# A fused cross-attention block in fp32: the pipeline's fifth step in an order of its own, and three smaller moves

## The chip, the cores and the metric

The kernel runs on one NeuronCore of one Trainium2 chip. The metric is the device time of one launch in microseconds. Each launch reads its inputs from the chip's memory (HBM) and writes the output there. TensorE is called PE in the profile, VectorE DVE, ScalarE ACT, GpSimd POOL, and SyncE, which does nothing here but issue transfers, SP.

## What is computed

For 128 batches of 128 tokens with 256 features, in fp32: 16-head attention of `x` on a second sequence `ctx`, whose mask lets token i see only tokens j < i, and whose row 0 is set to zero; the output projection, a residual and a layer norm; then a feed-forward block of 1024 hidden units with relu, a residual and a second layer norm.

```python
q = (x @ Wq + bq);  k = (ctx @ Wk + bk);  v = (ctx @ Wv + bv)      # 16 heads of 16
scores = where(j < i, q @ k.T / 4, -1e30)
attn = softmax(scores);  attn[:, :, 0, :] = 0
x1 = layer_norm(x + (attn @ v) @ Wo + bo, g1, be1)
out = layer_norm(x1 + relu(x1 @ W1 + b1) @ W2 + b2, g2, be2)
```

## The kernel before, in words

The work is cut into 64 pairs of batches, p = 0 to 63, and everything is written out by hand: each engine runs its instructions in the order in which the Python code emits them, and waits by semaphores where data or a buffer is not ready. So the order of the calls in `third`, `fourth`, `fifth`, `step` and `behind` is the order on every engine, and on SP the order in which transfers are issued.

A call of `step(p)` (L1114) handles four pairs at different stages:

- `weigh(p-2)` (L465) multiplies the older pair's transposed probabilities `pT` with its values into the PSUM tile `pc`, and `context` (L495) copies the result to `cxT` on ACT.
- `scores_both(p)` (L351) makes the scores `pss`. A query in the upper half of the tokens sees all 128 keys ("high", hi = 1), one in the lower half only 64 ("low"). The eight PSUM banks have fixed uses: high scores in banks 0 to 3, low scores in 6, 7, 4, 5.
- `mask`, `mask_high`, `low_maximum` (L377, L728, L742) add the mask and find the maxima on DVE; `exponential_by_head` (L746) makes 32 exponentials on ACT, the high ones straight from PSUM; `sums` (L405) adds them up on DVE and scales them on POOL.
- `queries(p+1)`, `keys(p+1)`, `values(p)` (L267, L277, L288) are the projections, each with PE products into a fixed bank (4, 0, 1) and copies by ACT (`qT`, `kT`, and `vz`, `vd` in `values_out`, L298).
- `attention_out(p-2)`, `attention_sum`, `attention_stats`, `shift`, `norm1` (L499 to L552) are the output projection `po` and the first layer norm.
- `hidden(p-3)` (L680) multiplies with W1 into `ph` and applies relu on ACT into `hT`. It needs the normalized tokens with features on the partitions, `x1T`: `turn_x1` (L652) transposes 32x32 blocks on DVE (`tbx`), and SP writes them to HBM in four transfers (`x1t`, L239) and reads them back in one (`x1T`, L242).
- `second_by_seven(p-4)` (L775) multiplies with W2 in seven quarter products instead of eight (Strassen's scheme in Winograd's form). `combine_hidden` (L764) makes the four sums of hidden blocks that it needs (`hS`), on two engines that are passed in. `sum_of_seven` (L803) adds the products up. `second_half` (L825) is the plain form for the first pairs.
- `turn(p, hi, t)` (L422) transposes blocks of the probabilities on DVE into the tile `tb`, in three calls for a pair: `(p,1,0)`, `(p,1,1)`, `(p,0,0)`. `bring` (L435) then issues sixteen transfers on SP that move `tb` to `pT`, the layout that `weigh` reads. Each reads columns that all three calls have written.
- `norm2`, `finish`, `store` (L579, L587, L597) are the second layer norm on ACT and POOL and the output transfer.

`sm` (scores and probabilities), `tb` and `pT` share four large buffers in turn (`wide`, L317), in the order in which the tiles are first asked for.

`empty(n)` (L213) puts n empty instructions into PE's stream. The kernel has 44 of them ahead of its first product (L839), which is a warm-up of twelve transposes of the identity, and one within each of the seven W2 products.

The first pairs are too early for this pattern. `third`, `fourth` and `fifth` (pairs 2, 3, 4) have orders of their own. The call `step(5)` has branches for `p == 5`: the store of pair 0, the second half of `hidden(2)`, `second_half(2, 0)`. `step(6)` has `second_half(2, 1)`. Behind the last pair, `behind(62)` and `behind(63)` (L1186) and some lines of their own finish the rest; there `combine_hidden` is split between DVE and POOL (`BOTH`).

The line numbers here and in the profile are those of the kernel before.

Of the kernel before, what the change touches and what calls it, by code (L numbers as in the profile page):

```python
# [19 lines left out]
def tile_cross_attention_block(  # L20
# [237 lines left out]
    def project(w, src, ps):  # L258
        for m in range(KC):
            for k in range(KC):  # L260
                nc.tensor.matmul(  # L261
                    ps[:, m * TP : (m + 1) * TP], w[:, k, m * P : (m + 1) * P], src[:, k, :],
                    start=(k == 0), stop=(k == KC - 1),
                )
        return ps
# [9 lines left out]
            )  # L275

    def keys(p):  # L277
        st = states[p]
        st["kT"] = proj.tile([P, KC, 2, TP], F32, tag="kT", name=f"kT_{p}")
        pk = project(wk, st["cT"], at_bank(0, f"pk_{p}") if p > 3 else bank(f"pk_{p}"))  # L280
        for m in range(KC):
            for e in range(2):
                nc.scalar.activation(  # L283
                    st["kT"][:, m, e, :], pk[:, m * TP : (m + 1) * TP], AF.Identity,
                    bias=bkh[:, m, e : e + 1], scale=half[:, e : e + 1],
                )

    def values(p):  # L288
        st = states[p]
        pv = st["pv"] = at_bank(1, f"pv_{p}") if p > 3 else bank(f"pv_{p}")  # L290
        for s in range(2):
            for k in range(KC):
                nc.tensor.matmul(  # L293
                    pv[:, s * D : (s + 1) * D], st["cT"][:, k, s * P : (s + 1) * P], wv[:, k, :],
                    start=(k == 0), stop=(k == KC - 1),
                )
# [300 lines left out]
    def store(p):  # L597
        nc.sync.dma_start(
            out[2 * p : 2 * p + 2].rearrange("b p d -> p b d"), states.pop(p)["t2"]
        )  # L600
# [76 lines left out]
            else:  # L677
                nc.scalar.copy(st["x1T"][:, :, :, k, :], pt[:, k])

    def hidden(p, fs, between=None):  # L680
        st = states[p]
        if fs[0] == 0:
            st["hT"] = ffn.tile([P, FC, TP], F32, tag="hT", name=f"hT_{p}", bufs=1)
        for f in fs[::2]:
            if p == 0:
                ph = bank(f"ph_{p}_{f}")
            else:
                ph = at_bank((2, 3, 4, 0)[f // 2], f"ph_{p}_{f}")
            for i in range(2):
                for k in range(KC):  # L690
                    nc.tensor.matmul(  # L691
                        ph[:, i * TP : (i + 1) * TP].rearrange("p (s i a) -> p s i a", s=2, a=32),
                        w1[:, k, (f + i) * P : (f + i + 1) * P], st["x1T"][:, :, :, k, :],
                        start=(k == 0), stop=(k == KC - 1),
                    )
            for i in range(2):
                nc.scalar.activation(  # L697
                    st["hT"][:, f + i, :], ph[:, i * TP : (i + 1) * TP], AF.Relu,
                    bias=(b1e_c if p else b1_c)[:, f + i : f + i + 1], scale=1.0,
                )  # L700
            if between:
                between(f)
# [133 lines left out]
        nc.vector.tensor_tensor(st["t2"][:, s], py[:, :D], st["x1b"][:, s], ALU.add)  # L836

    warm = bank("warm")
    empty(44)  # L839
    for i in range(12):  # L840
        nc.tensor.transpose(warm[:, i % 4 * P : (i % 4 + 1) * P], ident, ident)
    states[0] = {}
# [193 lines left out]
    def fourth():  # L1036
        p = 3
        load_ahead(p)
        scores(p, 1)
        mask(p, 1, A)  # L1040
        maximum(p, 1, ONE)
        second(0, 0)
        mask(p, 1, B)
        maximum(p, 1, TWO)
        exponential(p, 1, ONE)
        second(0, 1)
        tokens(p + 2, "c")
        sums(p, 1, ONE)
        exponential(p, 1, TWO)
        second_sum(0)  # L1050
        sums(p, 1, TWO)
        weigh(p - 1)
        context(p - 1)
        scores(p, 0)
        scale_w1()
        nc.gpsimd.tensor_tensor(b1e_c, b1e_c, b1_c, ALU.add)
        queries(p + 1)
        mask(p, 0, A)
        mask(p, 0, B)
# [12 lines left out]
        turn_x1(p - 1)  # L1072
        turn(p, 0, 0)
        bring(p, nc.sync, LATE_FIRST)
        stats(0, states[0]["t2"], 2)
        scale_and_shift(0)
        norm2(0)

    def fifth():
        p = 4  # L1080
        load_ahead(p)
        scores_both(p)
        mask(p, 0, B)
# [30 lines left out]
    def step(p):  # L1114
        last = p == NP - 1
        weigh(p - 2)
        context(p - 2)
        scores_both(p)
        if p > 6:
            combine_hidden(p - 4, POOL_ALONE)  # L1120
        if p == 5:
            second_sum(1)
            finish(0)
            store(0)
# [9 lines left out]
        if p > 5:  # L1134
            exponential_by_head(p, 0, range(H))
# [9 lines left out]
        if p == 5:  # L1145
            exponential_by_head(p, 0, range(H))
        values(p)
        values_out(p)
        if p > 5:
            norm2(p - 5)  # L1150
        sums(p, 1, ONE)
        sums(p, 1, TWO)
        sums(p, 0, ALL)
        turn_x1(p - 2)
        residual1(p - 3)
        if p > 6:
            second_by_seven(p - 4)
        elif p == 6:
            second_half(2, 1)
        hidden(p - 3, range(FC // 2 if p == 5 else 0, FC))  # L1160
        if p == 5:
            second_half(2, 0)
# [9 lines left out]
        if p > 5:  # L1172
            finish(p - 5)
            store(p - 5)
# [6 lines left out]
    for p in range(5, NP):  # L1181
# [96 lines left out]
```

## Time and profile before

| | us |
|---|---|
| median of 3 timed runs | 1550.86 (1549.78 to 1553.15) |
| time of the profiled execution | 1548.3 |
| its span, first to last instruction | 1546.2 |
| TensorE busy in it | 1518.6 (98%) |
| mean granted TensorE clock | 0.995 of full speed |

A row of the timeline has the start and the length in us, the engine, the line, the operation, the tile written and the tiles read, and how many instructions were merged; a bracket at its end gives the engine's idle time before the row and what is taken to have ended it. `SPq` rows are transfers being issued, not moved. A row of the waits has the waiting engine and tile, the releaser, the sum in us, the number of times and the longest. PEld is TensorE's weight load, which runs ahead of the products (PE), so its waits for the same thing can be longer.

### The profile page before, as it was taken

Reading aid. Unit: us, or ns where it says so; the run is one execution under the profiler, and the core shown is the slowest. Engines: PE = TensorE matmul, PEld = TensorE weight load, DVE = VectorE, ACT = ScalarE, POOL = GpSimd, SP = SyncE. Lnnn points to the kernel's source line nnn. Section 1 sums busy time; section 2 is a strip of 40 time slices with the busy share of each in tenths; the row PEclk is TensorE's granted clock in tenths of the full one; section 3 lists DMA queues with packets and bytes.
Section 4 is the critical chain, followed back from the end, with each engine's and each line's share of the span. In section 5 each row is a group of like instructions: output and inputs, shape, how many; then the busy total and the mean of one; then the engine's idle time right before and its main releaser. Section 6 shows DMA issues by size and latency. Waiting matters only on the chain.

```text
span 1546.2 us, 47890 instructions
## 1 busy us (share of the span) xinstructions
PE 1518.6 (98%) x17926; PEld 1362.5 (88%) x17926; DVE 1329.0 (86%) x2490; ACT 1119.8 (72%) x3391; POOL 1265.3 (82%) x1290
## 2 busy tenths in 40 slices
PE   8997999999999999999999999999999999999998
PEld 6786899899899899899899899899899899899887
DVE  6987889889889889889889889889898898898864
ACT  5666778778778778778778777777777777777752
POOL 6875888888888888888888888888888888888874
PEclk9998999999999999999999999999999999999999
DMA  8355666566556556556566566566566566555431
GB/s 198 77 116 125 145 133 143 124 139 143 138 134 147 124 135 146 138 137 147 117 141 147 133 138 135 135 136 150 132 136 140 127 137 151 131 132 130 107 94 48
DMA packets 415285, 204.24 MB, mean 132 GB/s; under 512 B 282448, under 2 KB 383056, under 8 KB 415056
## 3 DMA queue, kind: packets, MB, share of 16 engines
q1 hardware_dynamic: 413152, 200.13, 56.2%
q8 instruction: 144, 2.36, 0.7%
q10 hardware_dynamic: 1904, 1.06, 0.3%
q14 instruction: 85, 0.70, 0.2%
HBM read 70.26 MB, written 33.29 MB: 67 GB/s over the span
## 4 chain that ended last, share of the span: by engine, by line
PE 92%; POOL 3%; DVE 3%; issue 1%; ACT 1%; DMA 0%; POOLq 0%; DVEq 0%
PE ph L691 27%; PE py L784 13%; PE pz L784 10%; PE pq L261 8%; PE po L504 7%; PE pk L261 7%; PE pv L293 7%; PE pss L368 6%; PE pc L485 3%; PE pc L475 2%; POOL sm L415 1%; PE py L709 0%; DVE tb L428 0%; DVE sm L382 0%; POOL sd L525 0%
## 5 line engine op out<-in xcount | busy, mean ns | idle before, releaser
L691 PE MATMUL ph<-x1T,w 128*128 128x256 f32 x2048 | 455.6, 380 | 3.0 <-ACT kT L283 3.0
L691 PEld LDWEIGHTS ph<-x1T,w 128*128 128x128 f32 x2048 | 385.4, 191 | 54.3 <-ACT kT L283 3.4
L415 POOL TENSOR_TENSOR sm<-sm,rs 128x1024 f32<-128x1024 f32 x192 | 359.4, 1899 | 7.1 <-ACT hT L697 4.5
L752 ACT ACTIVATE sm<-pss,nmx 128x128 f32<-128x128 f32 x944 | 249.8, 415 | 131.5 <-DMA pT<-tb 84.5
L697 ACT ACTIVATE hT<-ph,b1e_c 128x256 f32<-128x256 f32 x504 | 209.5, 467 | 179.3 <-PE ph L691 179.1
L752 ACT ACTIVATE sm<-sm,nmx 128x64 f32<-128x64 f32 x944 | 231.8, 334 | 5.2
L413 DVE TENSOR_REDUCE su<-sm 128x8 f32<-128x1024 f32 (+1 forms) x192 | 225.9, 1176 | 9.4 <-ACT sm L752 5.6
L428 DVE STREAM_TRANSPOSE tb<-sm 128x1024 f32<-128x1024 f32 x186 | 220.8, 1214 | 0.0
L382 DVE TENSOR_TENSOR sm<-pss,neg 128x256 f32<-128x256 f32 (+1 forms) x276 | 108.3, 436 | 126.2 <-PE pss L368 118.6
L524 POOL TENSOR_SCALAR ve<-mv 128x2 f32<-128x2 f32 x127 | 29.4, 231 | 205.4 <-DVE mv L518 204.9
L784 PE MATMUL py<-wt,hS 128*128 128x128 f32 x1440 | 171.4, 275 | 3.1 <-POOL hS L771 3.1
L784 PEld LDWEIGHTS py<-wt,hS 128*128 128x128 f32 x1440 | 165.8, 192 | 3.7 <-POOL hS L771 3.7
L737 DVE TENSOR_REDUCE nmx<-pss 128x4 f32<-128x512 f32 x236 | 150.9, 681 | 0.0
L261 PE MATMUL pq<-xT,wq 128*128 128x256 f32 x504 | 127.2, 395 | 5.2 <-DVE sm L382 5.2
L283 ACT ACTIVATE kT<-pk,bkh,half 128x256 f32<-128x256 f32 x252 | 120.2, 557 | 3.9 <-PE pk L261 3.9
L293 PE MATMUL pv<-wv,cT 128*128 128x256 f32 x512 | 121.1, 379 | 1.6 <-ACT sm L752 1.6
L504 PE MATMUL po<-wo,cxT 128*128 128x256 f32 x512 | 121.2, 379 | 0.0
L261 PE MATMUL pk<-cT,wk 128*128 128x256 f32 x504 | 119.2, 379 | 0.0
L261 PEld LDWEIGHTS pq<-xT,wq 128*128 128x128 f32 x504 | 91.7, 192 | 26.0 <-issue 10.1
L293 PEld LDWEIGHTS pv<-wv,cT 128*128 128x128 f32 x512 | 97.1, 190 | 15.1 <-ACT sm L752 2.0
L504 PEld LDWEIGHTS po<-wo,cxT 128*128 128x128 f32 x512 | 97.0, 190 | 13.8 <-ACT cxT L497 0.3
L261 PEld LDWEIGHTS pk<-cT,wk 128*128 128x128 f32 x504 | 95.7, 190 | 13.1 <-issue 0.2
(131 smaller groups left out, 2971.5 us busy)
## 6 DMA issues: line engine op xcount, KB each, us to landing
pT<-tb SPq DMA_DIRECT2D x984, 96.0 KB
x1t<-tbx SPq DMA_DIRECT2D x252, 64.0 KB
x1T<-x1t SPq DMA_DIRECT2D x63, 256.0 KB
out_dram<-t SPq DMA_DIRECT2D x63, 256.0 KB
xb<-in_x_dram SPq DMA_DIRECT2D x124, 128.0 KB
cb<-in_ctx_dram SPq DMA_DIRECT2D x124, 128.0 KB
x<-in_x_dram SPq DMA_DIRECT2D x31, 512.0 KB
w<-in_L_xattn_W_dram SPq DMA_DIRECT2D x2, 1024.0 KB
```

The costliest lines, as they stand in the source:

```text
L261: nc.tensor.matmul(ps[:, m * TP : (m + 1) * TP], w[:, k, m * P : (m + 1) * P], src[:, k, :], start=(k == 0), stop=(k == KC - 1),)
L283: nc.scalar.activation(st["kT"][:, m, e, :], pk[:, m * TP : (m + 1) * TP], AF.Identity, bias=bkh[:, m, e : e + 1], scale=half[:, e : e + 1],)
L293: nc.tensor.matmul(pv[:, s * D : (s + 1) * D], st["cT"][:, k, s * P : (s + 1) * P], wv[:, k, :], start=(k == 0), stop=(k == KC - 1),)
L413: nc.vector.tensor_reduce(su, sm[:, part, :], AX.X, ALU.add)
L415: nc.gpsimd.tensor_tensor(sm[:, part, :], sm[:, part, :], rs[:, :, None].to_broadcast([P, part.stop - part.start, n]), ALU.mult,)
L428: nc.vector.transpose(st["tb"][:, :, at : at + 256].rearrange("p j (n a) -> p n j a", a=32), st["sm", hi].rearrange("p h j -> p (h j)")[:, ...
L504: nc.tensor.matmul(po[:, s * D : (s + 1) * D], cxT[:, k, s, :], wo[:, k, :], start=(k == 0), stop=(k == KC - 1),)
L691: nc.tensor.matmul(ph[:, i * TP : (i + 1) * TP].rearrange("p (s i a) -> p s i a", s=2, a=32), w1[:, k, (f + i) * P : (f + i + 1) * P], st[ ...
L697: nc.scalar.activation(st["hT"][:, f + i, :], ph[:, i * TP : (i + 1) * TP], AF.Relu, bias=(b1e_c if p else b1_c)[:, f + i : f + i + 1], sc ...
L737: nc.vector.tensor_reduce(st["nmx", 1][:, 4 * r : 4 * r + 4], st["sps", 1][r].rearrange("p (n j) -> p n j", j=P), AX.X, ALU.max, negate=True,)
L752: nc.scalar.activation(sm[:, h, :], src, AF.Exp, bias=nmx[:, h : h + 1], scale=1.0)
L784: nc.tensor.matmul(out, left(k), right(k), start=(k == 0), stop=(k == FC // 2 - 1))
```

## The change

Four things change. Nothing of the arithmetic does, apart from which engine makes some sums.

1. `step(5)` becomes `fall_in(5)`, with an order of its own. In `fifth` only the first of pair 4's three `turn` calls is left; the other two and `bring(4)` come behind `low_maximum(5)`. The low exponentials of pair 5 are split round the two W1 copies, the key copies come behind them (`keys` is cut into `project_keys` and `copy_keys`), and the W1 products use banks 2 and 3. `norm1(3)` comes late, and `turn_x1(3)` is no longer in this step. Two of pair 5's `turn` calls come at its end. In `step(6)`, the third `turn` of pair 5, `bring(5)` and `turn_x1(3)` follow the exponentials of pair 6, in this order.
2. In `fourth`, `queries(4)` comes ahead of `weigh(2)` and not behind `scores(3, 0)`.
3. At the end `combine_hidden` runs on DVE alone, and `finish` and `store` of an older pair come directly behind its `norm2`. In the last pair's step the values use bank 4 and not 1, and the second low mask comes ahead of the high ones.
4. The 44 empty instructions ahead of the warm-up are taken out; 44 are put between pair 1's W1 products, two or three behind each.

```diff
     def values(p):
-        pv = st["pv"] = at_bank(1, f"pv_{p}") if p > 3 else bank(f"pv_{p}")
+        pv = st["pv"] = at_bank(4 if p == NP - 1 else 1, f"pv_{p}") if p > 3 else bank(f"pv_{p}")
...
     def hidden(p, fs, between=None, banks=(2, 3, 4, 0)):
...
+                    if p == 1:
+                        empty(3 if f else 2)
...
-    empty(44)
...
     def fourth():
+        queries(p + 1)
         weigh(p - 1)
         context(p - 1)
         scores(p, 0)
...
-        queries(p + 1)
...
     def fifth():
         turn(p, 1, 0)
-        turn(p, 1, 1)
-        turn(p, 0, 0)
-        bring(p, nc.sync, LATE_FIRST)
         hidden(2, range(FC // 2))
...
+    def fall_in(p):
+        weigh(p - 2)
+        context(p - 2)
+        scores_both(p)
+        second_sum(1)
+        finish(0)
+        store(0)
+        add_bo(p - 1)
+        residual1(2)
+        load_ahead(p)
+        mask(p, 0, B)
+        mask_high(p, A)
+        exponential_by_head(p, 1, ONES)
+        mask_high(p, B)
+        exponential_by_head(p, 1, TWOS)
+        mask(p, 0, A)
+        low_maximum(p)
+        turn(p - 1, 1, 1)
+        turn(p - 1, 0, 0)
+        bring(p - 1, nc.sync, LATE_FIRST)
+        queries(p + 1)
+        exponential_by_head(p, 0, ONES)
+        attention_out(p - 2)
+        attention_sum(p - 2)
+        attention_stats(p - 2)
+        shift(p - 2, 1)
+        project_keys(p + 1)
+        values(p)
+        sums(p, 1, ONE)
+        sums(p, 1, TWO)
+        def between(f):
+            if f == 4:
+                exponential_by_head(p, 0, TWOS[:4])
+        hidden(2, range(FC // 2, FC), between, (2, 3, 2, 3))
+        exponential_by_head(p, 0, TWOS[4:])
+        copy_keys(p + 1)
+        values_out(p)
+        norm1(p - 2)
+        tokens(p + 2, "x")
+        tokens(p + 2, "c")
+        turn(p, 1, 0)
+        sums(p, 0, ALL)
+        turn(p, 1, 1)
+        second_half(2, 0)
+        stats(1, states[1]["t2"], 2)
+        scale_and_shift(1)
...
     def step(p):
+        if last:
+            mask(p, 0, A)
         mask_high(p, A)
...
+        if not last:
+            mask(p, 0, A)
         low_maximum(p)
+        exponential_by_head(p, 0, range(H))
+        if p == 6:
+            turn(p - 1, 0, 0)
+            bring(p - 1, nc.sync, LATE_FIRST)
+            turn_x1(p - 3)
...
-    BOTH = (nc.vector, nc.gpsimd)
+    VECTOR_ALONE = (nc.vector, nc.vector)
     def behind(p):
-        combine_hidden(p - 2, BOTH)
+        combine_hidden(p - 2, VECTOR_ALONE)
         norm2(p - 3)
+        finish(p - 3)
+        store(p - 3)
         second_by_seven(p - 2)
...
-        finish(p - 3)
-        store(p - 3)
...
-    combine_hidden(p - 1, BOTH)
+    combine_hidden(p - 1, VECTOR_ALONE)
```

More of the change, by code (lines that the diff above doesn't have):

```diff
@@ L277, in keys, with project_keys, copy_keys @@
     def keys(p):
+        project_keys(p)
+        copy_keys(p)
+    def project_keys(p):
         st = states[p]
         st["kT"] = proj.tile([P, KC, 2, TP], F32, tag="kT", name=f"kT_{p}")
-        pk = project(wk, st["cT"], at_bank(0, f"pk_{p}") if p > 3 else bank(f"pk_{p}"))
+        st["pk"] = project(wk, st["cT"], at_bank(0, f"pk_{p}") if p > 3 else bank(f"pk_{p}"))
+    def copy_keys(p):
+        st = states[p]
+        pk = st.pop("pk")
         for m in range(KC):
@@ L678, in turn_x1_on_pe, with hidden @@
                 nc.scalar.copy(st["x1T"][:, :, :, k, :], pt[:, k])
-    def hidden(p, fs, between=None):
+    def hidden(p, fs, between=None, banks=(2, 3, 4, 0)):
         st = states[p]
@@ L687, in hidden @@
             else:
-                ph = at_bank((2, 3, 4, 0)[f // 2], f"ph_{p}_{f}")
+                ph = at_bank(banks[f // 2], f"ph_{p}_{f}")
             for i in range(2):
@@ L1112, in tile_cross_attention_block @@
     POOL_ALONE = (nc.gpsimd, nc.gpsimd)
-    def step(p):
-        last = p == NP - 1
+    def fall_in(p):
         weigh(p - 2)
@@ L1118, in step @@
         scores_both(p)
[L1119 to L1124, printed above, removed]
+        second_sum(1)
+        finish(0)
+        store(0)
         add_bo(p - 1)
+        residual1(2)
         load_ahead(p)
@@ L1133, in step @@
         low_maximum(p)
-        if p > 5:
-            exponential_by_head(p, 0, range(H))
+        turn(p - 1, 1, 1)
[27 more added lines that the diff above has]
+        scale_and_shift(1)
+    def step(p):
+        last = p == NP - 1
+        weigh(p - 2)
+        context(p - 2)
+        scores_both(p)
+        if p > 6:
+            combine_hidden(p - 4, POOL_ALONE)
+        add_bo(p - 1)
[15 more added lines that the diff above has]
+            turn_x1(p - 3)
         if not last:
@@ L1144, in step @@
             keys(p + 1)
-        if p == 5:
-            exponential_by_head(p, 0, range(H))
         values(p)
         values_out(p)
-        if p > 5:
-            norm2(p - 5)
+        norm2(p - 5)
         sums(p, 1, ONE)
@@ L1157, in step @@
             second_by_seven(p - 4)
-        elif p == 6:
+        else:
             second_half(2, 1)
-        hidden(p - 3, range(FC // 2 if p == 5 else 0, FC))
-        if p == 5:
-            second_half(2, 0)
+        hidden(p - 3, range(FC))
         if p + 2 < NP:
@@ L1171, in step @@
         bring(p, nc.sync, LATE_FIRST)
-        if p > 5:
-            finish(p - 5)
-            store(p - 5)
+        finish(p - 5)
+        store(p - 5)
         stats(p - 4, states[p - 4]["t2"], 2)
@@ L1180, in tile_cross_attention_block @@
     fifth()
-    for p in range(5, NP):
+    fall_in(5)
+    for p in range(6, NP):
         step(p)
-    BOTH = (nc.vector, nc.gpsimd)
+    VECTOR_ALONE = (nc.vector, nc.vector)
     def behind(p):
```

## The prediction

> **What bounds the kernel now.** I read the page first: the busy times, the clock row and the chain that ended last. Then the busy times by step, a step being one pair of batches, counted from its weigh (the product of an older pair's probabilities and values, first on TensorE).
>
> ```profile
> PE 1518.6 (98%) x17926; PEld 1362.5 (88%) x17926; DVE 1329.0 (86%) x2490; ACT 1119.8 (72%) x3391; POOL 1265.3 (82%) x1290
> ...
> PEclk9998999999999999999999999999999999999999
> ...
> PE 92%; POOL 3%; DVE 3%; issue 1%; ACT 1%; DMA 0%; POOLq 0%; DVEq 0%
> ...
> 106.66:130.00 23.34, 20.33 (x226) 16.86 (x225) 14.08 (x27) 15.81 (x51) 15.40 (x14) 0.85 0.61 136
> 130.00:157.28 27.28, 22.08 (x242) 18.94 (x241) 24.44 (x45) 16.79 (x53) 14.94 (x18) 0.94 0.49 112
> 157.28:180.57 23.29, 23.29 (x282) 21.07 (x281) 20.49 (x39) 17.73 (x55) 20.79 (x21) 1.00 0.62 144
> ```
>
> The last three rows give length, then each engine's busy time and its count, then the granted clock. From 157.28 on a step is 23.29 us of TensorE without a hole, and the change leaves that loop alone. What can move is the start, the steps of pairs 5 and 6 (23.34 and 27.28 us, though each holds less work than a full step, at clocks of 0.85 and 0.94) and the end. The timeline shows where these two steps lose:
>
> ```profile
> 8.53 1.99 PE L865 MATMUL pk<-cT,wk 128*128 128x256 f32 x8
> 116.69 1.89 PE L691 MATMUL ph<-x1T,w 128*128 128x256 f32 x8
> 121.60 3.78 PE L691 MATMUL ph<-x1T,w 128*128 128x256 f32 x8 [3.01 <-ACT kT L283]
> 125.17 4.90 PE L830 MATMUL py<-w,hT 128*128 128x256 f32 x16
> 138.29 3.52 PE L261 MATMUL pq<-xT,wq 128*128 128x256 f32 x8 [5.20 <-DVE sm L382]
> 150.28 7.07 PE L691 MATMUL ph<-x1T,w 128*128 128x256 f32 x32
> ```
>
> The bracket holds the idle time and its releaser. In pair 5's step TensorE waits 3.01 for the copy of the keys, then runs eight products in 3.78 instead of 1.89 and sixteen in 4.90 instead of 3.54 (half of the 7.07 of 32): 3.01 + 1.89 + 1.36 = 6.3 us. In pair 6's step the queries wait 5.20 for VectorE's mask and run in 3.52 instead of 1.99: 6.7 us. So 13 us is the most that the new order can win there.
>
> **The change, part by part.** All times are in the frame of the profiled execution.
>
> *The fifth step.* The new order takes both waits away: the keys are copied behind the W1 results, and VectorE is through with the older pairs before pair 6's masks. TensorE would be done with pair 5's step at 118.4 + 1.8 + 3.5, about 124, instead of 130.0. But the order also moves two transposes of pair 4's probabilities (`turn(4,1,1)`, `turn(4,0,0)`) from ahead of pair 5's masks to behind its `low_maximum`. Each of the sixteen pT transfers of `bring(4)` reads what all three transposes write, so all of `bring(4)` goes with them, and `weigh(4)`, the first work of pair 6's step, needs all sixteen. In the same way `bring(5)` now stands behind `turn(5,0,0)`, behind pair 6's `low_maximum`; and `turn_x1(3)`, whose x1t transfers were issued ahead of `bring(5)` on SP (127.49 against 136.60), is put behind its sixteen. `hidden(3)`, the last work of pair 6's step, needs them. The rows that price this chain (for SP the second column is the time over which the line was issued):
>
> ```profile
> 79.32 2.36 DVE L428 STREAM_TRANSPOSE tb<-sm 128x1024 f32<-128x1024 f32 x2
> 108.94 0.76 DVE L382 TENSOR_TENSOR sm<-pss,neg 128x256 f32<-128x256 f32 x2 [0.90 <-PE pss L368]
> 114.11 1.22 DVE L744 TENSOR_REDUCE nmx<-sm 128x16 f32<-128x1024 f32 x1
> 111.55 1.27 POOL L590 TENSOR_TENSOR t<-t,be_r 128x512 f32<-128x512 f32 x1
> ...
> 65.97 6.03 SPq L443 DMA_DIRECT2D pT<-tb  x8
> 91.69 10.19 SPq L443 DMA_DIRECT2D pT<-tb  x16
> 107.53 11.86 SPq L443 DMA_DIRECT2D pT<-tb  x16
> 119.50 0.52 SPq L598 DMA_DIRECT2D out_dram<-t  x1
> 127.49 1.79 SPq L239 DMA_DIRECT2D x1t<-tbx  x4
> 136.60 10.12 SPq L443 DMA_DIRECT2D pT<-tb  x16
> 155.57 11.01 SPq L443 DMA_DIRECT2D pT<-tb  x16
> ...
> 73.70 0.30 PEld L475 LDWEIGHTS pc<-pT,vd 128*32 128x32 f32 x16 [2.33 <-DVE cT L247]
> 1520.66 1.90 SPq L239 DMA_DIRECT2D x1t<-tbx  x4
> 1526.74 7.14 PE L691 MATMUL ph<-x1T,w 128*128 128x256 f32 x32
> ```
>
> - Pair 5's masks start at 108.94 as before (VectorE waited for TensorE there) and end with the reduction at 115.33, 6.39 later. Two transposes of one pair cost 2.36: 117.7.
> - SP issues sixteen pT in 10.19, 11.86, 10.12 and 11.01, mean 10.8. Weigh(2) started 1.7 after the last issue (65.97 + 6.03 = 72.0, then 73.70). So weigh(4) starts at 117.75 + 10.8 + 1.7 = 130.25. SP is free by then: the store of pair 0 and the loads behind it can start when POOL has finished that pair, at 112.8, and before they took from 119.50 until ahead of 127.49; I estimate 4.3, from the store's 0.52 and loads of 0.7 to 0.8.
> - TensorE has idled from 124, longer than in either stall above. The mask follows the weigh by 2.28 (106.66 to 108.94) at full clock, by up to 4.56 at half of it. No row shows a weigh at half clock; I add 1.3, the middle, with 0 and 2.28 as bounds. Mask at 133.8, reduction done 6.39 later at 140.2, `turn(5,0,0)` 1.2: 141.4.
> - The sixteen issues of `bring(5)`: 152.2. From the first x1t issue to the product that needs its x1T took 6.1 at the end of the run (1520.66 to 1526.74, where TensorE had no more than that to wait). So `hidden(3)` starts at 158.3 and not at 150.28: 8.0 later.
> - TensorE has idled for 13 us. The half clock cost 1.5 (queries) and 1.89 + 1.36 = 3.2 after the shorter stalls; I add their mean, 2.4. Weigh(5) comes **10.4** later.
>
> Bounds: issues of 10.1, nothing lost in the weigh and 1.5 behind it give +6.9; issues of 11.9, 2.28 and 3.4 give +14.6.
>
> The Trainium skill, "TensorE: Matmul & The Clock Gate", Part 1, says that the array's clock is halved unless a window of about 3.4 us was busy, and again after an idle window, the windows running freely. The clocks of 0.85 and 0.94 above agree. By that rule work after a long idle time may run cold for up to two windows and lose 3.4 us: the step would be +11.4 and the whole sum 1.0 higher. The rule speaks against this change, which gives TensorE two longer idle times for two shorter ones.
>
> The rest of what the step issues (`finish(0)`, `residual1(2)`, the exponentials split round the W1 copies, `norm1(3)`) is the same work at other places, and TensorE's two waits cover it. Behind weigh(5) nothing is late: by the same terms pT(5) has landed at 154 and x1T(4) is issued by about 159, 24 ahead of its use.
>
> *The start.*
>
> ```profile
> 1.10 0.29 POOL masks.py:199 TENSOR_SCALAR_AFFINE_SELECT ident<-ident 128x128 f32<-128x128 f32 x1
> 4.10 2.79 PE L841 MATMUL warm<-ident 128*128 128x128 f32 x12 [4.10 <-POOL half L185]
> 6.47 0.87 PEld L228 LDWEIGHTS ptc<-ident,c_first 128*128 128x128 f32 x4
> ```
>
> The identity is ready at 1.39, yet TensorE starts at 4.10, behind 44 empty instructions. Without them the twelve warming transposes end 2.7 earlier; the next ones then wait for an input whose landing no row gives, and may be gapped and keep the half clock: pk in up to 3.8 and not in 1.99. Between -2.7 (the input is there) and +1.9 (nothing gained, pk at half clock); I take **-1.0**, since the transposes at 6.47 follow the warming ones without a gap, so their input was there by then. In pair 1's W1 products the 44 cost 0: the gapless step holds seven among its products too. At most 2.7, what they hold up at the start.
>
> *Queries of pair 4.*
>
> ```profile
> 75.39 0.58 ACT L497 COPY cxT<-pc 128x508 f32<-128x508 f32 x1
> 77.83 1.89 PE L504 MATMUL po<-wo,cxT 128*128 128x256 f32 x8
> 90.06 1.95 DVE L382 TENSOR_TENSOR sm<-pss,neg 128x256 f32<-128x256 f32 x4 [0.39 <-PE pss L368]
> ```
>
> They fill part of the 2.33 us that weigh(2) waits (row 73.70). Their copy, some 0.8, goes ahead of the context's copy at 75.39, so the output product starts at about 77.0: 0.8 earlier. That reaches pair 4's masks, but VectorE, which waited 0.39 for them, can use no more: **-0.4**, between 0 and -0.8.
>
> *The end.*
>
> ```profile
> 1463.86 0.76 DVE L382 TENSOR_TENSOR sm<-pss,neg 128x256 f32<-128x256 f32 x2 [3.21 <-PE pss L368]
> 1484.28 0.78 DVE L770 TENSOR_TENSOR hS<-hT 128x512 f32<-128x512 f32 x1 [0.33 <-ACT hT L697]
> 1489.46 1.86 PEld L784 LDWEIGHTS py<-wt,hS 128*128 128x128 f32 x16 [1.04 <-POOL hS L771]
> 1502.02 1.47 DVE L770 TENSOR_TENSOR hS<-hT 128x512 f32<-128x512 f32 x1 [1.21 <-ACT hT L697]
> 1501.67 1.27 POOL L590 TENSOR_TENSOR t<-t,be_r 128x512 f32<-128x512 f32 x1
> PEld py L784 <- POOL hS L771: 3.7, 3, 2.1
> PEld pv L293 <- ACT sm L752: 2.0, 1, 2.0
> ```
>
> The last pair's values wait 2.0 for exponentials that read bank 1; in bank 4 they wait for a mask done at 1464.6, ahead of them. Three W2 products wait 3.7 for combinations on POOL. On VectorE four take 0.78 each, 3.1 from 1484.28 on; the last is needed at 1489.46 - 1.04 + 1.86 - 2.0 = 1488.3, 4.0 from there. **-5.7** in all. The Trainium skill, "SBUF — State Buffer", "SBUF: two separate sides", says that a VectorE operation with two SBUF inputs is blocked for the whole of a GpSimd operation; the 1.47 beside POOL's 1501.67 row agrees. Were all four that long, the last would be 1.9 late: between -3.8 and -5.8.
>
> **Sum.** 10.4 - 1.0 - 0.4 - 5.7 = +3.3 us. The profiled execution took 1548.3 us: 1551.6. The median shown, 1550.86, stands 2.6 above it, and I put the difference on the median: **1554.2 us**, 0.21% slower.
>
> **The rivals.**
> 1. *The same chain at its low ends* (issues of 10.1, little half clock, the start's whole gain): from 6.9 - 2.7 - 0.8 - 5.8 = -2.4 to +3.1, say 1552. For it: 10.12, the shortest issue row, had no load just ahead of it.
> 2. *x1T(3) is not late* (the other side, faster). The place is SP's queue behind pair 6's reduction. Were x1t(3) issued ahead of 139, `hidden(3)` would start when TensorE is ready, about 145, weigh(5) would come 5.2 earlier than before, and the sum is -12: 1539. Against it: SP issues in order, at 0.6 us or more each, and the reduction itself ends at 140.
> 3. *Neither wait appears*, and the order does what it is for: -13 - 1.4 - 5.7 = -20: 1531. It needs pT(4) by 124, sixteen issues in 4.5 us. No row comes near.
>
> **How the numbers follow.** A measurement tells about 0.2%, 3.1 us, from no change. The forecast's chain from +3.1 to +12 has a chance of 0.51, rival 1 of 0.37, rivals 2 and 3 of 0.06 each. The first two are one mechanism, parted by half clock and issue times. Faster 0.12, same 0.37, slower 0.51. The range from 1549.0 to 1561.0 holds nearly all of rival 1 and the forecast up to +10; it leaves out the fast rivals and the far end.
>
> **What would show it.** Pair 6's weigh waits about 6 us for pT; sixteen pT lines stand just ahead of x1t(3) on SP; `hidden(3)` waits about 13 us for x1T; the clock row dips in the slices round 130 and 160. At the end there is no wait for hS and none of pv for an exponential; warm starts before 2 us. I am wrong if weigh(4) starts before 126, if hidden(3) starts within 16 us of it, or if a later step is not 23.29.

## The result, and the profile after

| | before | after |
|---|---|---|
| median of 17 timed runs each, taken together, us | 1550.93 (1546.93 to 1553.15) | 1553.62 (1550.79 to 1558.30) |
| ratio of the times, 95% interval | | 1.0017 (1.0009 to 1.0025) |
| time of the profiled execution | 1548.3 | 1554.08 |
| its span | 1546.2 | 1552.4 |
| mean granted TensorE clock in it | 0.995 | 0.991 |

The changed kernel is slower by 0.17%, 2.6 us with an interval from 1.4 to 3.9. The predicted time was 1554.2.

In the changed kernel's code the lines are shifted: the weigh is L483 and L493, scores L376, W1 L699, the four sums of `combine_hidden` L780 to L783, `sum_of_seven` L823 and L831, pT transfers L451, output stores L606. From its page, the busy times, the clock row and the engines of the chain that ended last:

```profile
PE 1518.0 (98%) x17926; PEld 1361.9 (88%) x17926; DVE 1334.9 (86%) x2496; ACT 1121.2 (72%) x3391; POOL 1261.0 (81%) x1284
...
PEclk9997999999999999999999999999999999999999
...
PE 92%; DVE 4%; DMA 2%; SPq 1%; issue 1%; ACT 1%; POOL 0%; ACTq 0%; POOLq 0%; DVEq 0%
```

The shares hardly differ from those of before. One digit of the clock row does: the fourth slice, 116 to 155 us, stood at 8 and stands at 7. The busy times by step, cut at the weighs of pairs 3, 4, 5 and 6 as before:

```profile
104.50:128.30 23.80, 17.11 (x226) 14.85 (x226) 18.97 (x35) 15.86 (x51) 18.85 (x20) 0.95 0.59 129
128.30:165.28 36.98, 24.30 (x240) 20.63 (x240) 20.18 (x37) 17.14 (x53) 14.12 (x16) 0.76 0.47 107
165.28:188.57 23.29, 23.29 (x281) 21.07 (x280) 20.52 (x38) 17.76 (x55) 18.26 (x16) 1.00 0.50 113
```

Pair 6's step takes 36.98 instead of 27.28, at a clock of 0.76; the loop behind it still takes 23.29 a step. Four differences of weigh times make the whole:

- The weigh of pair 3 comes 2.2 earlier (104.50, 106.66): the start and the queries.
- The weigh of pair 5 comes 8.0 later (165.28, 157.28), so the fall-in costs 10.2.
- The weigh of pair 61 comes 7.9 later (1469.52, 1461.58): the loop changes nothing.
- From there to the end of the span it is 82.9 instead of 84.6: the end gains 1.7.

Together 6.2, the difference of the two spans. The timeline of the changed kernel at its start and in the fall-in:

```profile
1.45 2.82 PE L850 MATMUL warm<-ident 128*128 128x128 f32 x12 [1.45 <-POOL ident masks.py:199]
...
4.63 1.11 PE L228 MATMUL ptc<-ident,c_first 128*128 128x128 f32 x4 [0.37 <-DMA c_first<-in_ctx_dram]
...
6.53 1.99 PE L874 MATMUL pk<-cT,wk 128*128 128x256 f32 x8
...
128.30 0.65 PE L483 MATMUL pc<-pT,vd 128*32 128x64 f32 x16 [6.69 <-DMA pT<-tb]
...
132.29 0.76 DVE L390 TENSOR_TENSOR sm<-pss,neg 128x256 f32<-128x256 f32 x2 [6.22 <-PE pss L376]
...
116.40 10.10 SPq L451 DMA_DIRECT2D pT<-tb  x16
...
139.93 10.11 SPq L451 DMA_DIRECT2D pT<-tb  x16
139.79 0.67 DVE L663 STREAM_TRANSPOSE tbx<-x 128x512 f32<-128x512 f32 x1
150.14 1.99 SPq L239 DMA_DIRECT2D x1t<-tbx  x4
...
156.60 8.75 PE L699 MATMUL ph<-x1T,w 128*128 128x256 f32 x32 [12.68 <-DMA x1T<-x1t]
```

Both waits are where the prediction put them: 6.69 for pT(4), 12.68 for x1T(3). SP stands between them: sixteen pT transfers, and the x1t transfers only when those are issued. VectorE had written `tbx` of pair 3 by 140.46, 9.7 before the first of its transfers was issued. The end of the changed kernel:

```profile
1491.28 10.58 SPq L451 DMA_DIRECT2D pT<-tb  x16
1501.97 1.05 SPq L606 DMA_DIRECT2D out_dram<-t  x2
...
1504.47 0.69 DVE L823 TENSOR_TENSOR t<-x1b,py 128x512 f32<-128x512 f32 x1 [3.38 <-DMA out_dram<-t]
...
1506.69 0.55 DVE L831 TENSOR_TENSOR t<-t,pz 128x384 f32<-128x384 f32 x1
...
1507.35 0.43 PE L483 MATMUL pc<-pT,vd 128*32 128x64 f32 x16 [1.29 <-issue]
...
1526.38 1.59 POOL L569 TENSOR_TENSOR x1b<-x1b,be1b_r 128x512 f32<-128x512 f32 x1
...
1526.78 1.75 DVE L781 TENSOR_TENSOR hS<-hT 128x512 f32<-128x512 f32 x1
...
1530.25 1.16 PE L794 MATMUL py<-wt,hS 128*128 128x128 f32 x8 [0.51 <-DVE hS L782]
```

Two things here were not in the prediction. The sums of pair 60 write the buffer from which pair 58's result is still to be stored; that store is issued on SP only behind the sixteen pT transfers, so the sums wait 3.38. (They are issued in the step of pair 62's weigh; three of my expectations below, those of end_only, hs_only and both_store, call them the sums of pair 62.) The last weigh writes PSUM bank 7, which the last of these sums reads until 1507.24, and it starts at 1507.35, 1.29 late, though its own transfers were issued by 1501.86. And the very last combinations take 1.57 to 1.75 each beside operations of GpSimd, not 0.7, so that W2 products wait for hS three times, 0.48, 0.51 and 0.52. In the kernel before, the same store came just in time; from its timeline:

```profile
1493.68 0.52 SPq L598 DMA_DIRECT2D out_dram<-t  x1
...
1496.12 0.69 DVE L813 TENSOR_TENSOR t<-x1b,py 128x512 f32<-128x512 f32 x1
```

Issue to sum is 2.4 here and 2.5 after, but VectorE had its own work until 1496.07, so nothing was lost.

### The profile page after: what moved, and what is told of

It is laid out like the page before. It is cut to its first block, busy times and chain, and to the rows that moved or that the text cites. A ratio compares the mean times of both kernels' runs of the same rounds, so it can differ in the third digit from the quotient of the medians.

```text
span 1552.4 us, 47881 instructions
## 1 busy us (share of the span) xinstructions
PE 1518.0 (98%) x17926; PEld 1361.9 (88%) x17926; DVE 1334.9 (86%) x2496; ACT 1121.2 (72%) x3391; POOL 1261.0 (81%) x1284
## 4 chain that ended last, share of the span: by engine, by line
PE 92%; DVE 4%; DMA 2%; SPq 1%; issue 1%; ACT 1%; POOL 0%; ACTq 0%; POOLq 0%; DVEq 0%
PE ph L699 28%; PE py L794 13%; PE pz L794 10%; PE pq L261 7%; PE po L512 7%; PE pv L301 7%; PE pk L261 6%; PE pss L376 6%; PE pc L493 4%; PE pc L483 2%; SPq L451 1%; DVE su L421 1%; DMA x1T<-x1t 0%; PE py L719 0%; DMA pT<-tb 0%
## 5 line engine op out<-in xcount | busy, mean ns | idle before, releaser
L699 PE MATMUL ph<-x1T,w 128*128 128x256 f32 x2048 | 455.3, 380 | 12.8 <-DMA x1T<-x1t 12.7
L699 PEld LDWEIGHTS ph<-x1T,w 128*128 128x128 f32 x2048 | 385.4, 191 | 64.4 <-issue 13.2
```

The source lines that it names most:

```text
L699: nc.tensor.matmul(ph[:, i * TP : (i + 1) * TP].rearrange("p (s i a) -> p s i a", s=2, a=32), w1[:, k, (f + i) * P : (f + i + 1) * P], st[ ...
```

## The experiments

Each kernel was timed beside the kernel before on the same chip. My theory: the new order loses its time at two places on SP's queue, pT(4) behind the late transposes and x1t(3) behind `bring(5)`, and the other edits gain about what the trace says. The rivals are the clock and VectorE's order.

**x1T of pair 3 ahead (x1t_ahead).** From the changed kernel:

```diff
     def fall_in(p):
         turn(p, 1, 1)
+        turn_x1(p - 2)
...
     def step(p):
             bring(p - 1, nc.sync, LATE_FIRST)
-            turn_x1(p - 3)
```

> The changed kernel with one move: the transposition of pair 3's x1 and its five transfers are issued at the end of pair 5's step, ahead of the sixteen pT transfers of pair 5, instead of behind them. My theory, that the queue of SP sets the start of pair 3's W1 products: they start when TensorE is ready, about 144 to 146 in the frame of the changed kernel and not at 156.6; then the weigh of pair 5 waits for its own transfers (last issue 150.1, plus 1.7) and starts at about 152 to 153 instead of 165.3; the whole becomes 12 to 13 us shorter, about 1541. Rival, that the step is long because TensorE's clock is down and VectorE is behind: the products start earlier but run at half clock, and the weigh of pair 5 moves by 5 us or less, about 1549.

Measured: 1540.65, ratio to the kernel before 0.9932 (0.9919 to 0.9944), 13.0 less than the changed kernel's median. Its timeline:

```profile
127.39 2.00 SPq L239 DMA_DIRECT2D x1t<-tbx  x4
...
140.76 10.88 SPq L451 DMA_DIRECT2D pT<-tb  x16
...
145.01 7.07 PE L699 MATMUL ph<-x1T,w 128*128 128x256 f32 x32
153.32 0.43 PE L483 MATMUL pc<-pT,vd 128*32 128x64 f32 x16 [1.25 <-DMA pT<-tb]
```

The products start when TensorE is ready, at full clock (7.07), and the next weigh waits 1.25 for its own transfers: the wait of 12.68 was SP's queue. The rival is out. It is also what the prediction's second rival would have given, had its condition held.

**pT of pair 4 early (pt4_early).** The other move undone, again from the changed kernel:

```diff
     def fifth():
         turn(p, 1, 0)
+        turn(p, 1, 1)
+        turn(p, 0, 0)
+        bring(p, nc.sync, LATE_FIRST)
...
     def fall_in(p):
         low_maximum(p)
-        turn(p - 1, 1, 1)
-        turn(p - 1, 0, 0)
-        bring(p - 1, nc.sync, LATE_FIRST)
```

> The changed kernel with the other move undone: the last two transposes of pair 4's probabilities and its sixteen pT transfers are issued in pair 4's own step again. My theory: the weigh of pair 4 loses its wait of 6.7 us and starts at about 122 instead of 128.3; the masks of pair 6 follow at 2.3 instead of 4.0; the whole chain behind them (reduction, last transpose, sixteen transfers, x1T of pair 3) comes 8 us earlier, so pair 3's W1 products start at about 148.5 and the weigh of pair 5 at about 157: 8 us shorter, about 1545.5, with the wait for x1T still there. Rival, that the two waits are one stall that only moves: VectorE, charged again with 2.4 us of transposes ahead of pair 5's masks, gives them later, and the weigh of pair 5 stays within 3 us of 165.3, about 1551 to 1554.

Measured: 1545.69, ratio 0.9969 (0.9957 to 0.9981), 7.9 less than the changed kernel. Its timeline:

```profile
121.47 0.43 PE L483 MATMUL pc<-pT,vd 128*32 128x64 f32 x16
...
131.72 10.12 SPq L451 DMA_DIRECT2D pT<-tb  x16
...
148.44 9.47 PE L699 MATMUL ph<-x1T,w 128*128 128x256 f32 x32 [12.71 <-DMA x1T<-x1t]
```

The weigh starts without a wait, the chain behind it comes 8.2 earlier (139.93 to 131.72), and the second wait is as long as it was, 12.71. The two waits add up; neither hides the other.

**Both moves (both).** The two diffs above together.

> The changed kernel with both moves of the two earlier runs: pair 4's last two transposes and its transfers in its own step, and pair 3's x1 turned and transferred ahead of pair 5's sixteen pT transfers. My theory, that these two places on SP are all that the new order loses: weigh of pair 4 at about 121.5, last transpose of pair 5 done at 131.4, sixteen issues to 142.2, weigh of pair 5 at about 144 instead of 165.3: 21 us shorter than the changed kernel, about 1532.5, and 18 shorter than the kernel before. Rival, that the two gains of 7.9 and 13.0 overlap, because VectorE takes back what it is given: 13 to 15 shorter, about 1539.

Measured: 1534.0, ratio 0.9890 (0.9876 to 0.9903), 19.6 less than the changed kernel and 16.9 less than the kernel before. Its timeline:

```profile
121.54 0.43 PE L483 MATMUL pc<-pT,vd 128*32 128x64 f32 x16
...
124.11 0.71 DVE L663 STREAM_TRANSPOSE tbx<-x 128x512 f32<-128x512 f32 x1 [1.49 <-ACT x L554]
...
126.39 0.76 DVE L390 TENSOR_TENSOR sm<-pss,neg 128x256 f32<-128x256 f32 x2 [0.19 <-DMA x1t<-tbx]
...
137.34 7.07 PE L699 MATMUL ph<-x1T,w 128*128 128x256 f32 x32
146.33 0.43 PE L483 MATMUL pc<-pT,vd 128*32 128x64 f32 x16 [1.92 <-DVE mv L526]
```

The weigh of pair 5 comes at 146.3 and not at the 144 expected: pair 6's mask starts 4.9 behind the weigh, at 126.39, since VectorE first waits 1.49 for x1(3) to turn. Of 7.9 and 13.0 all but 1.3 adds up. So the whole change is worth 16.9 us once these two groups of transfers are issued early again, as in the kernel before. The traces show 14.3 of it: 2.2 ahead of the weigh of pair 3, 8.8 from there to the weigh of pair 5, 3.3 at the end. This is the prediction's third rival, 1531, with its condition met.

**TensorE kept at work in its waits (kept_busy, kept_busy_longer).** Transposes of the identity that nobody reads fill the two waits of the changed kernel (54 and 100 in the second run, for 22 and 48):

```diff
     def weigh(p):
+        if p == 4:
+            for i in range(22):
+                nc.tensor.transpose(pc[:, i % 4 * P : (i % 4 + 1) * P], ident, ident)
...
     def hidden(...):
+            if p == 3 and f == 0:
+                fill = at_bank(7, "fill")
+                for i in range(48):
+                    nc.tensor.transpose(fill[:, i % 4 * P : (i % 4 + 1) * P], ident, ident)
```

> The changed kernel with TensorE kept at work while it waits: 22 transposes of the identity ahead of the weigh of pair 4 (about 5 us of its wait of 6.7) and 48 ahead of pair 3's W1 products (about 10.5 of 12.7). They are extra work that nobody reads. Theory, that the prediction's two half-clock terms (1.3 at the weigh, 2.4 at the end of the step) are a cost of their own: weigh, scores and W1 products run at full clock, the weigh of pair 5 comes 3 to 3.7 us earlier, about 1550.3. Rival, that the clock falls for another reason than the idle time: the products stay at half clock, 0, or up to 1.5 later by the extra work.

Measured: 1556.3, ratio 1.0027 (1.0015 to 1.0039). My count was wrong: a transpose took 0.11, so waits of 4.11 and 6.82 stayed, and TensorE came out of both at half clock. This run leaves the question open.

> As the run before of this kind, whose transposes took 0.11 each and not the 0.22 assumed, so that waits of 4.1 and 6.8 stayed and the clock fell in both: now 54 transposes (6.3) ahead of the weigh of pair 4 and 100 (11.3) ahead of pair 3's W1 products, so that under 1 us of waiting should be left at each. Theory, half clock is a cost of its own that follows the idle time: granted clock 1.00 from 105 to 190, the weigh of pair 4 in 1.5 and not 2.7, masks 1.7 earlier, W1 products in 7.1 and not 8.7, the weigh of pair 5 3 us earlier than in the changed kernel: about 1550.5. Rival: the clock falls all the same, 0.

Measured: 1552.9, ratio 1.0011 (1.0003 to 1.0020), which its interval doesn't part from the changed kernel's 1.0017. The timeline of this second run, whose lines are shifted again (the weigh is L486, W1 L706):

```profile
127.70 0.43 PE L486 MATMUL pc<-pT,vd 128*32 128x64 f32 x16 [0.31 <-DMA pT<-tb]
...
129.98 0.75 DVE L390 TENSOR_TENSOR sm<-pss,neg 128x256 f32<-128x256 f32 x2 [4.03 <-PE pss L376]
...
147.79 3.71 SPq L239 DMA_DIRECT2D x1t<-tbx  x4
...
155.88 8.83 PE L706 MATMUL ph<-x1T,w 128*128 128x256 f32 x32 [3.61 <-DMA x1T<-x1t]
```

Half of the theory is shown. With 0.31 of waiting left, the weigh runs at full clock and the mask follows it by 2.28; in the changed kernel it followed by 3.99 (128.30 to 132.29). Half clock cost 1.7 there. The other half failed: the four x1t transfers, ready 2.4 earlier, were issued over 3.71 and not 1.99, a wait of 3.6 came back, and the W1 products took 8.83. One of the four issues took 2.17 by itself, where the others took 0.5; no row names a reason.

**Start and queries alone (start_queries),** on the kernel before:

```diff
-    empty(44)
...
+                    if p == 1:
+                        empty(3 if f else 2)
...
     def fourth():
+        queries(p + 1)
         weigh(p - 1)
...
-        queries(p + 1)
```

> The kernel before with the empty instructions moved from the start into pair 1's W1 products and the queries of pair 4 ahead of the second context, nothing else. From the changed kernel's trace (weigh of pair 3 at 104.50 instead of 106.66): 2.2 us shorter than the kernel before. The prediction's terms gave 1.4. Rival: the waits of pair 5's and pair 6's steps, set by VectorE, take the gain back, 0 to 1.

Measured: 1547.12, ratio 0.9980 (0.9970 to 0.9989), 3.1 by the ratio (1.7 to 4.7); its trace has the weigh of pair 3 at 104.49, 2.2 earlier, as the changed kernel has. The gain isn't taken back.

**The kernel before once more (before_again).**

> The kernel before once more, for a second profile: the profiled execution shown first took 1548.3 where the median is 1550.9. If the difference lies in the clock of pair 5's and 6's steps, the weigh of pair 5 comes later than 157.3 and the end is as long as before (84.6 from the weigh of pair 61 to the end of the span); if it lies at the end, the end is 86 to 88.

Measured: 1550.33 in its profiled execution, span 1548.3. The end took 84.9, 0.3 more than in the first profile. The weigh of pair 5 came at 159.12 instead of 157.28, but not for pair 5's or 6's step: the loss is there already at the weigh of pair 3, 108.66 instead of 106.66. First the kernel before in the profile shown at the beginning, then in this one:

```profile
73.73 0.43 PE L475 MATMUL pc<-pT,vd 128*32 128x64 f32 x16 [1.96 <-DMA x1t<-tbx]
73.95 0.66 PE L485 MATMUL pc<-pT,vz 128*32 128x64 f32 x32
...
75.21 0.69 PE L340 MATMUL pss<-kT,qT 32*64 32x128 f32 x32
```

```profile
74.36 0.43 PE L475 MATMUL pc<-pT,vd 128*32 128x64 f32 x16 [1.98 <-DMA pT<-tb]
74.58 0.90 PE L485 MATMUL pc<-pT,vz 128*32 128x64 f32 x32
...
76.69 1.16 PE L340 MATMUL pss<-kT,qT 32*64 32x128 f32 x32
```

The same program and the same wait of 2.0: once the clock stays, once it halves half a microsecond into the weigh, and the step is 1.4 longer; the other 0.6 was lost ahead of this weigh. The queries, put into this wait, leave 0.28 of it. So the edit that I priced at 0.4 also takes away a loss that comes in some executions and not in others: in one of the two here, and in none of end_only, pv_only and hs_only below, which begin like the kernel before.

The record of the granted clock shows more. Until the kernel's end, half clock comes in stretches of 3.41 us or a multiple of it, on a grid that lies differently in each execution. In this profile the clock is at 0.50 from 74.84 to 78.25, and the stretch ahead of that, 71.43 to 74.84, holds the whole wait. In the first profile the grid has an edge at 73.14, inside the wait, and the clock stays. Laid over TensorE's rows (PE and PEld) of all fourteen traces, a stretch at full clock in which it idled for 2.0 or more was always followed by half clock, one with 1.7 or less never; in between both occurred, with 1.95 here and 1.95 in pv_only.

The Trainium skill, "TensorE: Matmul & The Clock Gate", Part 1, says that the windows run freely and that the same kernel therefore differs from run to run; the two traces agree. Its idle window of 3.4 us doesn't fit: here 2.0 was enough.

**The end alone (end_only, pv_only, hs_only),** on the kernel before. end_only has all of the diff's edits in `values`, the mask order, `behind` and the lines after it; pv_only has the bank and the mask order, hs_only has the two lines `combine_hidden(..., VECTOR_ALONE)`.

> The kernel before with only the end's edits: the last pair's values in bank 4, its mask order, both combinations of the end on VectorE, finish and store of the end ahead of the W2 products. The prediction's term: 5.7 us shorter than the kernel before. By the changed kernel's trace, where a wait for the output store delays the sums of pair 62 and with them the last weigh, and where the last combinations run beside GpSimd: 1.8 shorter. Rival: that the store's wait is an accident of the changed kernel's phase and is absent here: 3 to 4 shorter.

> The kernel before with only the last pair's values in bank 4 and its mask order. The wait of 2.0 goes: 1.8 shorter by the traces of the changed kernel and of the run with all edits of the end (step of 19.9 instead of 21.7). If the edits of the end together are worth 5.1 by the medians and this one is worth more than 2.5 here, then the wait also cost the kernel before something beside itself, such as a clock halved after it in part of the executions.

> The kernel before with only the two combinations of the end on VectorE; finish and store stay where they were. Prediction's term: 3.7 shorter. By the traces, where four combinations at the very end take 1.6 to 1.8 each beside GpSimd and the products still wait 0.9: 2.3 shorter (0.85 at the first, 1.4 at the second). Rival, that finish and store had to move too, since the sums of pair 62 wait for the store: 1 shorter.

Measured: end_only 1545.65, ratio 0.9969 (0.9957 to 0.9981); pv_only 1551.38, 1.0007 (0.9998 to 1.0015); hs_only 1547.44, 0.9981 (0.9973 to 0.9990). From the weigh of pair 61 to the end of the span the traces have 81.6, 86.7 and 83.2, against 84.6 and 84.9 in the two of the kernel before. The wait for the store is there in end_only too (3.44 ahead of the sums of pair 60), so the rival's reason is out, though the end is 3.0 shorter in the trace, as it said, and not 1.8. Taking the wait of the values away is worth nothing by itself. The timeline of pv_only:

```profile
1488.79 1.26 POOL L771 TENSOR_TENSOR hS<-hT 128x512 f32<-128x512 f32 x1
...
1490.11 3.53 PE L784 MATMUL py<-wt,hS 128*128 128x128 f32 x16 [2.83 <-POOL hS L771]
```

Its step of pair 63 is 1.8 shorter (19.9), but GpSimd is no earlier: the W2 products wait 2.83 instead of 0.85, and run at half clock behind that wait, 3.53 instead of 2.05. From hs_only to end_only, with the combinations on VectorE in both, the gain is 1.8 by the medians, which their intervals don't part, and 1.6 by the traces; the moves of `finish` and `store` are in this difference too. In hs_only all three waits for hS are gone, 3.1 together, and a wait of 2.35 for the last x1T takes much of that back.

**The store on another queue (both_store),** from both:

```diff
-        store(p - 3)
+        store(p - 3, nc.scalar)      # in behind; store passes the queue on
```

> The kernel with both moves and, at the end, the two stores of the second-last pairs issued on ScalarE's queue instead of behind the sixteen pT transfers on SP. Theory, that the sums of pair 62 wait 3.4 for that store, and the last weigh waits 1.1 to 1.4 for those sums because it writes the PSUM bank that they read: both waits go, 1.1 to 1.3 shorter than with both moves alone, about 1532.8. Rival, that the bank has nothing to do with it and the last weigh waits for its pT: the wait for the store goes and that of the weigh stays, 1534.

Measured: 1534.68, ratio 0.9893 (0.9878 to 0.9908), no gain. Its timeline:

```profile
1473.10 13.91 SPq L451 DMA_DIRECT2D pT<-tb  x16
...
1481.13 0.41 ACTq L606 DMA_DIRECT2D out_dram<-t  x1
...
1483.42 0.69 DVE L823 TENSOR_TENSOR t<-x1b,py 128x512 f32<-128x512 f32 x1 [0.51 <-DMA out_dram<-t]
...
1485.64 0.55 DVE L831 TENSOR_TENSOR t<-t,pz 128x384 f32<-128x384 f32 x1
...
1489.07 0.43 PE L483 MATMUL pc<-pT,vd 128*32 128x64 f32 x16 [1.18 <-DMA pT<-tb]
```

The edit moves the stores of pairs 59 and 60; pair 58's stays on SP and is issued at 1487.11. The sums of pair 60 now wait 0.51, for pair 59's store: the semaphore that they wait for is that store's, so they get its buffer here. They end at 1486.19, before TensorE is ready for the weigh (1487.89): the bank no longer holds it. But the sixteen issues took 13.91, where they took 10.36 in the run with both moves. The last six of them start at 1483.32, when the store has landed: the eleventh transfer counts on the same one of eight semaphores as the store and waits for it. The weigh waits 1.18 for pT instead. One wait replaced the other at the same length, as the rival had it in time but not in its reason. That the bank was what held the last weigh rests on the eight traces with the combinations and the stores moved and the stores on SP (the changed kernel, x1t_ahead, pt4_early, end_only, both, the two with TensorE kept at work, and quiet_end): in each it starts 0.1 behind the end of that sum.

**Nothing on GpSimd beside the last combinations (quiet_end),** from both:

```diff
-    residual1(p)
-    finish(p - 2)
-    store(p - 2)
     sum_of_seven(p - 1)
+    residual1(p, nc.vector)
+    finish(p - 2, nc.vector)
+    store(p - 2)
```

> The kernel with both moves, and at its end four operations of GpSimd (the scaled x1 of the last pair, the finish of pair 61) put on VectorE behind the sums of pair 62, where VectorE has nothing else. Theory, that the last combinations take 1.6 to 1.8 instead of 0.7 because GpSimd works beside them on the same memory: all four take 0.7, the two waits of 0.4 and 0.5 ahead of the last W2 products go, 0.9 shorter than with both moves alone, about 1533.1. Rival, that they are long for another reason (their operands, the ScalarE write just ahead of them): they stay at 1.6 to 1.8 and the time at 1534.0.

Measured: 1533.26, ratio 0.9885 (0.9868 to 0.9902); the median doesn't part it from both, its trace does (80.2 from the weigh of pair 61 to the end, against 81.3):

```profile
1507.17 0.68 DVE L781 TENSOR_TENSOR hS<-hT 128x512 f32<-128x512 f32 x1
1507.77 0.69 DVE L782 TENSOR_TENSOR hS<-hS,hT 128x512 f32<-128x512 f32 x1
...
1508.33 2.84 PE L794 MATMUL py<-wt,hS 128*128 128x128 f32 x24
```

The same operations on the same operands take 0.68 once GpSimd is quiet, and no product waits. The Trainium skill, "SBUF — State Buffer", "SBUF: two separate sides", says that a VectorE operation with two SBUF inputs and a GpSimd operation that reads SBUF lock each other out; 0.68 against 1.75 agrees.

## Why the prediction was right, and where it was not

| term, us | predicted | trace of after | runs |
|---|---|---|---|
| fall-in | +10.4 | +10.2 | +10.5 |
| start | -1.0 | -2.0 | -3.1 with the queries |
| queries of pair 4 | -0.4 | -0.2 | |
| end | -5.7 | -1.7 | -4.8 (-6.7 to -2.9) |
| sum | +3.3 | +6.2 | +2.6 (+1.4 to +3.9) |

The last column takes the ratios of start_queries, end_only and the changed kernel times 1551; the fall-in is what then remains, if the parts add. It is a remainder and no measurement of its own.

**The fall-in** was right in mechanism and size. With the two early gains taken off (1.4), the chain put the weigh of pair 4 at 128.9, `bring(5)` at 140.0, the W1 products at 156.9; they came at 128.30, 139.93 and 156.60. The issues took 10.1 instead of 10.8, the way from x1t to the products 6.5 instead of 6.1, half clock 1.7 at the weigh instead of 1.3. At the end of the step it cost 1.7 (8.68 from the first W1 product to the next weigh, 7.0 at full clock), where I had 2.4. The granted clock was at a half until 159.87, 3.3 into these products. The rule of two windows, my estimate from the Trainium skill, "TensorE: Matmul & The Clock Gate", Part 1, allowed up to 3.4 there; the trace has half of it. x1t_ahead and pt4_early show the two places separately. None of the three signs of being wrong came: the weigh of pair 4 started at 128.30, the W1 products 28.3 later, and a later step is 23.29.

**The start** gained 2.0, between the -1.0 taken and the bound of -2.7: pk starts at 6.53 instead of 8.53 and at full clock, since its input came 0.4 behind the warming transposes. Of the 2.65 by which these start earlier, that wait and the gap behind it took 0.65.

**The queries** gained 0.2 in this trace, as small as predicted. What the step missed is the clock: the wait that they fill halved it in one of two executions of the kernel before.

**The end** is the step that failed. In the trace the values' wait went (the step of pair 63 is 1.8 shorter), but of the 3.7 for combinations only a part: four at 0.78 was right twice and wrong the third time, beside GpSimd, where they took 1.57 to 1.75. That was the bound of -3.8, which I named with the Trainium skill's rule of the two sides ("SBUF — State Buffer", "SBUF: two separate sides") and then left aside. The sign that there would be no wait for hS failed with it. And a wait came that I had not seen, for a store that the change doesn't move. I summed the waits removed and did not ask what is late next.

The price of the removed waits was about right: in quiet_end the end takes 80.2, and without the 0.99 that its last weigh still waits it would take 79.2, 5.4 less than 84.6. The changed kernel loses 3.7 of that again: 1.3 ahead of the last weigh, and 2.4 from there to the end of the span, which takes 45.05 instead of 42.62 in quiet_end, where GpSimd is quiet beside the combinations. The 1.7 of the trace is what remains. In the kernel before, the sums of pair 60 started 12.8 behind the weigh of pair 62 (1496.12, 1483.30) and the store had just landed; without the values' wait TensorE is 1.8 earlier against SP, and the store, behind `bring(63)`, is not. In six other kernels with the same edits of the end the traces show a gain of 2.4 to 3.3, and the runs of end_only give 4.8. Traces and runs meet only at the edge of the interval; that the kernel before now and then loses clock at its end too, as pv_only does, would explain the rest, but no trace of it shows that.

**The way to the median** hid this error. I added the 2.6 by which the first profile of before stood below the median. Its second profile was 2.0 longer, 1.4 of it by the half clock at the weigh of pair 2, and the change removes that wait; the changed kernel's own profile stands 0.5 above its median. Had I been right about the end and the start, the sum of the parts would have been 6.2, and with 2.6 added 1557.1. Two errors, the end 4.0 too good and the median 3.1 too bad, nearly cancel. So it is luck that the time came out within 0.6; the mechanism that decides the sign was right.

## What to carry to other kernels

When a program order moves a transfer, write out the in-order queue that it is issued on: here a small transfer behind sixteen others cost 13 us at one place, and a store behind sixteen others 1.3 at another, while the rest of the order gained. A change that looks neutral can be the sum of a large gain and two large losses, so try its pieces singly before giving it up; this one was worth 16.9 us as a whole with two pieces put back. And a removed wait is only worth its length if the next operand is early too: the values' wait alone gave nothing, and, with `finish` and `store` moved too, about 1.7 once the combinations were early.

## What the runs showed of the hardware

- A TensorE wait of 2.0 was followed by half clock in one execution and not in another of the same program. A wait of 3.01 for the key copy in pair 5's step was followed by half clock in the first profile and not in that of end_only, whose program is the same up to there: the same eight products took 3.78 and 1.99. Behind waits of 3.6 to 12.7 the next products were at half clock in every trace shown here. Where it could be told apart, half clock cost 1.4 to 3.2 behind one wait. In these traces it followed when about 2 us of one 3.41 us stretch of the clock's grid were idle.
- VectorE sums of two SBUF operands of 128x512 took 0.68 alone and, in the changed kernel's last combinations, 1.57 to 1.75 beside GpSimd operations; these took 1.59 to 1.71 instead of 1.27.
- A transfer on ScalarE's queue held up SP's issues by 3.6, through a semaphore that both use in turn, though their data have nothing to do with each other.
